# The first attention and the first plain feed-forward of a network of eight steps, put into one order of work written out by hand

## The chip, the core and the metric

The kernel runs on one core of a Trainium2 chip. A core has TensorE for matrix products (its weight loads are shown as PEld), VectorE (DVE), ScalarE (ACT), GpSimd (POOL) and the queues that issue transfers. Each engine works through its own list of instructions in order, and waits where an operand is not there yet. The metric is the device time of one execution in microseconds; less is better. Three runs of the kernel before took 3157.12, 3162.74 and 3170.88 us.

## The reference

The input is a tensor `x` of 2 batches, 1024 tokens and 256 channels in float32. Eight steps add to it in turn:

```python
x = x + attn_a(layernorm(x))     # 16 query heads, 8 key heads of 32, soft cap
x = x + ffn0(layernorm(x))       # 256 -> 512 -> 512 -> 256, relu
x = x + attn_b(layernorm(x))     # 16 query heads, 4 key heads of 16
x = x + ffn0(layernorm(x))       # the same weights again
x = x + attn_d(layernorm(x))     # differential attention
x = x + ffn1(layernorm(x))       # quantized weights
x = x + ttt(layernorm(x))        # a recurrence over chunks of 16 tokens
x = x + ffn1(layernorm(x))
```

Only the first two lines are touched by the change. The attention projects the normalized tokens to queries, keys and values, turns queries and keys by a rotary table, and forms for every head

```python
att = softmax(where(causal, 50 * tanh(q @ k.T / 16 / 50), -inf))
y = (att @ v) @ Wo
```

The feed-forward is `relu(relu(h @ W1.T + b1) @ W2.T + b2) @ W3.T + b3`.

## The kernel before

`build` (L1763) loads `x` (16 tiles of 128 tokens) and all weights of the first four steps at the start, on the queues of SP and ScalarE, and then runs the list `STAGES` (L1760): the first attention, the feed-forward, the second attention, the feed-forward again, and so on. The feed-forward `ffn0` is one function, called twice.

**The attention** (`attn_a`, L310, and `attn_a_chunk`, L360). The work is cut into four chunks: for each batch the first 512 queries (c = 0) and the last 512 (c = 1). The manual order of `in_order` (L277) makes TensorE, VectorE, ScalarE and GpSimd follow the order in which the code is written. A chunk consists of rounds, one for each pair (u, r) of head groups and each block kb of 128 keys. Four heads are worked at a time, on four row groups of TensorE. Chunk c = 0 has 16 rounds, chunk c = 1 has 32, and in the last four rounds of each head group only 512, 384, 256 and 128 query columns are left by the causal mask.

A round has three parts. `scores` (L424) forms four score products (L431) into two PSUM tiles of two banks, then ScalarE takes tanh (L437) out of PSUM and exp (L442) in place, in two halves, and GpSimd zeroes what the mask forbids (L445) where the block lies on the diagonal. `weigh` (L450) forms the products of the weights with v (L456) into the PSUM bank `py`, and VectorE adds the weights to a running sum `acc` (L466 to L473). At the last block of a head group `finish` (L478) forms row sums with a column of ones (L483), and VectorE turns, divides and turns back (L488 to L494) into `yT`.

Between the rounds stand pieces: the inputs of the next chunk and the outputs of the chunk before. The inputs of a pair of tiles are the layernorm in three steps (`token_inputs`, L293: `stats` and `rows` on VectorE with scalings on GpSimd, L196 and L205; `turn` with transposes on TensorE, L220, and a copy on VectorE, L223), then for each tile `queries`, `keys`, `turn_queries` and `turn_keys`: a projection (L232), the rotary products on VectorE (L259, L268) and their sum on GpSimd (L273), transposes (L396, L405) and copies (L397, L406). The outputs are four products with Wo (L411), each added to `x` on VectorE (L416). `spread` (L282) gives each round a number of pieces by its columns. The loop at L342 issues for round n: its scores, one piece, the products with v of round n−1, the finish of round n−2 if it was the last of its group, and the remaining pieces.

PSUM has eight banks here: four for the score tiles, two for the pieces (tag `g`), one for `py` and one for the row sums (`sm`).

**The feed-forward** (`ffn0`, L520) starts when the attention has ended, and its order is left to the planner. `layernorm_T` (L137) takes statistics of eight tiles (L146, L147), a square root on ScalarE (L148), scales on VectorE (L154), transposes on TensorE (L160) and copies on both engines in turn. Then, for each quarter of 512 tokens, two hidden layers of four blocks each (products L537 with two and four steps; relu with bias on ScalarE, L541) and four outputs (L546), added to `x` on VectorE (L551), with the bias b3 added on GpSimd (L552).

**The second attention** (`attn_b`) allocates its own memory and PSUM, clears some of it on GpSimd (L574 to L587), takes its first two tiles through a layernorm, and goes on in an order of its own.

Of the kernel before, what the change touches and what calls it, by code (L numbers as in the profile page):

```python
# [44 lines left out]
class Net:  # L45
# [235 lines left out]

    def spread(self, weights, pieces):  # L282

        total, at, out = sum(weights), 0.0, []
        done = 0
        for w in weights:
            at += w
            upto = round(len(pieces) * at / total)
            out.append(pieces[done:upto])
            done = upto  # L290
        return out
# [18 lines left out]
    def attn_a(self, w, wo, cos, sin):  # L310
# [6 lines left out]
        with ExitStack() as ctx:  # L317
# [8 lines left out]
            for b in range(B):  # L326


                kT = big.tile([P, 2, T], F32, tag="kT", name="kT", bufs=2)
                v = big.tile([P, NB, 8, 32], F32, tag="v", name="v", bufs=2)  # L330
                chunks += [self.attn_a_chunk(pools, b, c, kT, v) for c in range(2)]
            for step in chunks[0].inputs:
                step()
            rounds, fill = [], []
            for n, chunk in enumerate(chunks):
                inputs = chunks[n + 1].inputs if n + 1 < len(chunks) else []
                outs = chunks[n - 1].outputs if n else []
                pieces = []
                interleave_into(pieces, inputs, [lambda: None] * 2 + outs if outs else [])
                fill += self.spread([r.columns for r in chunk.rounds], pieces)  # L340
                rounds += chunk.rounds
            for n in range(len(rounds) + 2):  # L342
                here, last, ended = (
                    rounds[n - j] if 0 <= n - j < len(rounds) else None for j in range(3)
# [6 lines left out]
                if last:  # L351
                    last.weigh()
# [4 lines left out]
            for step in chunks[-1].outputs:  # L357
                step()

    def attn_a_chunk(self, pools, b, c, kT, v):  # L360
# [7 lines left out]
        def bank(name):  # L368
            return ps.tile([P, 512], F32, tag="g", name=name, bufs=2)

        def queries(j, made):
            if j == 0:
                shared["qT"] = big.tile([P, 2, 2, 512], F32, tag="qT", name="qT", bufs=2)
                shared["yT"] = big.tile([P, 4, 512], F32, tag="yT", name="yT", bufs=2)
# [3 lines left out]
            qr = roped["q"] = work.tile([P, 2, 2, 4, HD], F32, tag="qr", name="qr")  # L378
# [5 lines left out]
        def keys(j, made):  # L384
# [3 lines left out]
            kr = roped["k"] = work.tile([P, NKV, HD], F32, tag="kr", name="kr")  # L388
            self.rope(work, pkv[:, 0:256], NKV, HD, cos[:, i, :], sin[:, i, :], True,
                      [(kr, lambda t: t)], "rq", 2)  # L390
            nc.vector.tensor_copy(v[:, i], pkv[:, 256:512].rearrange("p (h d) -> p h d", d=HD))

        def turn_queries(j):
            pt = bank("t_ps").rearrange("p (n q) -> p n q", q=P)
            for n in range(4):
                nc.tensor.transpose(pt[:, n, :], roped["q"][:, n // 2, n % 2], self.ident)  # L396
# [4 lines left out]
        def turn_keys(j):  # L401
            i = 4 * c + j
            pt = bank("t_ps").rearrange("p (n q) -> p n q", q=P)
            for u in range(2):
                nc.tensor.transpose(pt[:, u, :], roped["k"][:, 4 * u : 4 * u + 4, :], self.ident)  # L405
            nc.vector.tensor_copy(kT[:, :, i * P : (i + 1) * P], pt[:, 0:2])  # L406
# [11 lines left out]
        def round_(u, r, kb):  # L418
# [5 lines left out]
            def scores():  # L424
# [4 lines left out]
                for s in range(4):  # L429
                    rows = slice(32 * s, 32 * s + 32)  # L430
                    nc.tensor.matmul(  # L431
                        tiles[s // 2][:, s % 2, 0:m], kT[rows, u, kb * P : (kb + 1) * P],
# [17 lines left out]
            def weigh():  # L450
# [4 lines left out]
                for s in range(4):  # L455
                    nc.tensor.matmul(  # L456
                        py[32 * s : 32 * s + 32, off:512], v[:, kb, 4 * u + s, :],
# [16 lines left out]
                if kb == end:  # L474
                    own.turned = work.tile([P, 16, 32], F32, tag="tny", name="turned")
                    nc.vector.transpose(own.turned.rearrange("p n d -> p (n d)"), py)

            def finish():  # L478


                sm = ps.tile([P, 512], F32, tag="sm", name="sm")
# [23 lines left out]
        chunk.outputs = [lambda j=j: output(j) for j in range(4)]  # L505
        chunk.inputs = []
        for p in range(2):
            made = {}
            i = b * NB + 4 * c + 2 * p
            chunk.inputs += self.token_inputs(work, bank, (i, i + 1), made)  # L510
            for j in (2 * p, 2 * p + 1):
                chunk.inputs += [
                    lambda j=j, m=made: queries(j, m), lambda j=j, m=made: keys(j, m),
                    lambda j=j: turn_queries(j), lambda j=j: turn_keys(j),
# [1398 lines left out]
```

## Time and profile before

| what | value |
| --- | --- |
| runs of the kernel before | 3157.12, 3162.74, 3170.88 us |
| the profiled execution, its time | 3170.71 us |
| its span, first to last instruction | 3168.9 us |
| mean granted clock of TensorE | 0.89 of full speed |
| first attention, first scores to last output | 55.1 to 431.4 us |
| first feed-forward, to its last product | 431.7 to 555.9 us |
| first transposes of the second attention | 563.0 us |

A line of TensorE's or another engine's timeline gives the start, the length, the engine, the line of the code and the operation with its result and operands; "x8" means eight instructions in a row, merged. A float32 product is two instructions in the trace, so a round's four score products show as eight. A line of waits gives the engine and the line that waited, what ended the wait, the total in microseconds, how often, and the longest. "PE py L456 <- POOL pr L445" is TensorE, at the products with v, standing idle until GpSimd's mask was done. In the view by stretches each engine has its busy time and, in brackets, the number of its instructions. Matrix products overlap in the record, so the distance from one start to the next tells more of their cost than their lengths.

### The profile page before, as it was taken

The page shows a single profiled execution, that of the slowest core. Times are in us where ns is not written, and L with a number is a line of the kernel's source. Part 1 is how long each engine was busy: PE and PEld are TensorE (multiplying, and loading weights), DVE is VectorE, ACT ScalarE, POOL GpSimd, SP SyncE. Part 2 cuts the span into 40 slices and gives each one's busy share as a digit, 9 for nine tenths or more (in the row PEclk, how much of TensorE's full clock was granted, in tenths as well). Part 3 has the DMA queues.
Part 4 walks back from the last instruction along what each step waited for, and adds up shares of the span by engine and source line. Part 5 has one row for each costly group of instructions (what it writes and reads, how often), then busy time and mean ns, then how long its engine had stood idle before and what let it go on. Part 6 is the DMA issues. An engine that isn't in the chain of part 4 may idle for free.

```text
span 3168.9 us, 66877 instructions
## 1 busy us (share of the span) xinstructions
PE 2640.7 (83%) x26384; PEld 1622.8 (51%) x26384; DVE 1922.1 (61%) x6646; ACT 1355.2 (43%) x2713; POOL 1030.5 (33%) x1648
## 2 busy tenths in 40 slices
PE   6888889699997866978887878878867689889998
PEld 2233245343433433655655555555644567767777
DVE  4776650576765446666676867778615665665652
ACT  2785942144454334664655555656512121221210
POOL 2444210211203456566564655656500000000000
PEclk8999989799998975988989888898987699999999
DMA  3000000000001100000000000000001111001000
GB/s 111 1 1 1 1 1 0 1 1 1 1 1 27 47 8 1 1 1 1 1 1 1 1 1 1 1 1 1 1 18 22 30 23 22 10 22 36 22 10 14
DMA packets 61978, 35.38 MB, mean 11 GB/s; under 512 B 43216, under 2 KB 58080, under 8 KB 61664
## 3 DMA queue, kind: packets, MB, share of 16 engines
q1 hardware_dynamic: 59472, 29.49, 3.6%
q8 instruction: 208, 3.41, 0.4%
q10 hardware_dynamic: 2192, 1.61, 0.2%
q14 instruction: 106, 0.87, 0.1%
HBM read 22.68 MB, written 8.39 MB: 10 GB/s over the span
## 4 chain that ended last, share of the span: by engine, by line
PE 36%; DVE 13%; ACT 7%; issue 4%; POOL 3%; DMA 0%; POOLq 0%; DVEq 0%; ACTq 0%; SPq 0%
PE ph L1255 6%; PE po L1746 4%; DVE p L1057 4%; PE e L1046 4%; ACT p L1068 4%; PE pg L1733 4%; PE pu L1733 3%; PE dT L1105 3%; PE po L1272 2%; POOL p L1081 2%; DVE p L1094 2%; PE py L1122 1%; PE pa L1416 1%; PE kh L1416 1%; PE pq L1416 1%
## 5 line engine op out<-in xcount | busy, mean ns | idle before, releaser
L1057 DVE CUSTOM_DVE_ANT_0 p<-e,mask 128x512 f32<-128x512 f32 (+3 forms) x768 | 381.7, 553 | 106.4 <-PE e L1046 105.1
L1068 ACT ACTIVATE p<-p,nm 128x128 f32<-128x128 f32 (+7 forms) x512 | 389.9, 764 | 97.7 <-DVE nm L1057 88.1
L1081 POOL TENSOR_SCALAR p<-p,ra,neg_lam 128x128 f32<-128x128 f32 (+7 forms) x256 | 222.8, 870 | 235.6 <-DVE ra L1077 180.9
L1105 PE MATMUL dT<-ident,p 128*128 128x128 f32 x1152 | 200.5, 308 | 112.9 <-ACT pT L1109 29.7
L1109 ACT ACTIVATE pT<-dT 128x128 f32<-128x128 f32 (+7 forms) x256 | 165.5, 647 | 285.8 <-PE dT L1105 284.5
L1046 PE MATMUL e<-kT,qT 32*128 32x512 f32 (+3 forms) x1536 | 234.2, 625 | 28.0 <-DVE nm L1057 26.7
L196 POOL TENSOR_SCALAR ln_mv<-ln_mv 128x2 f32<-128x2 f32 x48 | 15.7, 328 | 739.9 <-DVE ln_mv L194 728.3
L1094 DVE CUSTOM_DVE_ANT_0 p<-p,rs 128x128 f32<-128x128 f32 (+7 forms) x256 | 207.8, 833 | 69.8 <-POOL p L1085 69.6
L1105 PEld LDWEIGHTS dT<-ident,p 128*128 128x128 f32 x1152 | 154.7, 158 | 173.2 <-POOL p L1085 49.5
L723 ACT ACTIVATE pr<-s 128x512 f32<-128x512 f32 (+3 forms) x384 | 157.1, 496 | 167.6 <-PE s L718 164.4
L1098 POOL TENSOR_SCALAR p<-p,md 128x128 f32<-128x128 f32 (+7 forms) x256 | 208.2, 813 | 25.4
L437 ACT ACTIVATE pr<-s 128x1024 f32<-128x1024 f32 (+1 forms) x192 | 146.1, 821 | 126.7 <-PE s L431 123.1
L1255 PE MATMUL ph<-xT,up 128*128 128x256 f32 x512 | 138.2, 419 | 20.0 <-DVE inter L1263 18.3
L683 PE MATMUL s<-kT,qT 32*128 32x512 f32 (+3 forms) x768 | 151.2, 531 | 2.3 <-ACT pr L723 1.3
L442 ACT ACTIVATE pr<-pr 128x1024 f32<-128x1024 f32 (+1 forms) x192 | 153.0, 861 | 0.0
L1255 PE MATMUL ph<-xT,gate 128*128 128x256 f32 x512 | 138.5, 417 | 15.8 <-ACT xT L225 10.8
L691 DVE CUSTOM_DVE_ANT_0 masked<-s,mask 128x128 f32<-128x128 f32 (+3 forms) x256 | 110.7, 487 | 55.0 <-PE s L683 54.6
L1746 PE MATMUL po<-down,inter 128*128 128x256 f32 x512 | 140.7, 437 | 2.2 <-DVE x L1753 1.2
L445 POOL TENSOR_SCALAR_AFFINE_SELECT pr<-pr 128x256 f32<-128x256 f32 x128 | 93.5, 747 | 146.0 <-ACT pr L442 84.4
L1733 PE MATMUL pg<-xT,gate 128*128 128x256 f32 x512 | 131.3, 401 | 7.5 <-ACT xT L225 5.5
L456 PE MATMUL py<-pr,v 128*32 128x512 f32 (+3 forms) x768 | 115.1, 541 | 26.6 <-POOL pr L445 24.6
L1255 PEld LDWEIGHTS ph<-xT,up 128*128 128x128 f32 x512 | 101.2, 207 | 62.3 <-DVE inter L1263 28.9
(301 smaller groups left out, 5440.1 us busy)
## 6 DMA issues: line engine op xcount, KB each, us to landing
uk_d<-uk SPq DMA_DIRECT2D x128, 32.0 KB, 1.8
r<-uk_d SPq DMA_DIRECT2D x8, 512.0 KB, 4.2
x<-in_L_attn_a_X SPq DMA_DIRECT2D x4, 512.0 KB, 6.1
qh_d<-qh SPq DMA_DIRECT2D x8, 256.0 KB, 2.7
o<-qh_d SPq DMA_DIRECT2D x128, 16.0 KB, 1.8
out<-x SPq DMA_DIRECT2D x4, 512.0 KB, 3.1
w<-in_L_ffn_W2T SPq DMA_DIRECT2D x1, 1024.0 KB, 7.9
pk<-in_L_ffn_gate_packed SPq DMA_DIRECT2D x8, 128.0 KB, 2.4
```

The source lines that it names most:

```text
L723: nc.scalar.activation(pr[:, g, off:512], tiles[g][:, 0:m], AF.Exp, scale=0.25)
L1046: nc.tensor.matmul(own.tiles[h][:, a, 0 : hi - lo], made["q"][r : r + 32, a, t, :], kT[r : r + 32, a, lo:hi], start=True, stop=True,)
L1057: nc.vector.tensor_tensor_reduce(own.p[h][a][:, lo:hi], own.tiles[h][:, a, 0 : hi - lo], neg_row[:, T - nk + lo : T - nk + hi], -1.0, 3e38 ...
L1068: nc.scalar.activation(own.p[h][a], own.p[h][a], AF.Exp, bias=own.nm[:, h, a : a + 1], scale=-1.0, accum_out=own.sm[:, h, a : a + 1],)
L1081: nc.gpsimd.tensor_scalar(p1, p1, own.ra[:, h : h + 1], nlam[:, head : head + 1], ALU.mult, ALU.mult)
L1094: nc.vector.tensor_tensor_reduce(p0, p0, p1, own.rs[:, h, 0:1], -3e38, ALU.add, ALU.max, md)
L1098: nc.gpsimd.tensor_scalar(p0, p0, md, 1.0, ALU.add, ALU.mult)
L1105: nc.tensor.transpose(dT[:, kb, :], own.p[h][0][:, kb * P : (kb + 1) * P], self.ident)
L1109: nc.scalar.activation(pT[:, 0 : qb + 1, :], dT[:, 0 : qb + 1, :], AF.Exp)
L1255: nc.tensor.matmul(ph[:, j, :], w[:, kc, m * P : (m + 1) * P], f.xT[:, kc, :], start=(kc == 0), stop=(kc == 1),)
L1733: nc.tensor.matmul(ph[:, j, :], m_[:, kc, m * P : (m + 1) * P], f.xT[:, kc, :], start=(kc == 0), stop=(kc == 1),)
L1746: nc.tensor.matmul(f.po[:, b], inter[m // 2][:, m % 2, b * P : (b + 1) * P], wd[:, m % 2, (m // 2) * C : (m // 2 + 1) * C], start=(m == 0) ...
```

## The change

The first attention and the first feed-forward become one function, `attn_a_ffn0`, in one order written out by hand, and the list of stages has one entry less. The feed-forward's second call stays as it was.

- The feed-forward is cut into 22 pieces for each quarter of 512 tokens (`ffn0_pieces`): twice stats, rows and turn of a pair of tiles (the bias b3 is added to `x` in rows, on GpSimd); four pieces of the first hidden layer; eight of the second, each with two of a block's four steps; four outputs. The layernorm is that of `token_inputs`, without ScalarE. Relu with bias is one VectorE instruction that adds and takes the maximum with 0.
- Every piece has a cost. `share` gives out the pieces of a chunk by cost, with weights of the rounds' columns plus 100. A first part of the next chunk's inputs goes to the first three rounds of a chunk; the rest, mixed with the outputs of the chunk before and the pieces of the feed-forward, to the others. The first quarter of the feed-forward stands in the second chunk, the second and most of the third in the fourth. Nine pieces of the third quarter, the outputs of the last chunk and the last quarter follow after the last round.
- The products with v of round n−2, not n−1, are issued in round n, and the finish of round n−3.
- The row sums lose their own PSUM bank, and the pieces have three banks instead of two, which the sums share.
- In the inputs of a pair of tiles the order is now queries 0, keys 0, queries 1, transposes of queries 0, keys 1, transposes of keys 0, of queries 1, of keys 1. Keys and values are kept per chunk instead of per batch, in three buffers.

The core of the diff:

```diff
-            for n, chunk in enumerate(chunks):
-                inputs = chunks[n + 1].inputs if n + 1 < len(chunks) else []
-                outs = chunks[n - 1].outputs if n else []
-                pieces = []
-                interleave_into(pieces, inputs, [lambda: None] * 2 + outs if outs else [])
-                fill += self.spread([r.columns for r in chunk.rounds], pieces)
+            for chunk, first, second, third in (
+                (chunks[0], chunks[1].inputs, [], []),
+                (chunks[1], chunks[2].inputs, chunks[0].outputs + after[0], []),
+                (chunks[2], chunks[3].inputs, chunks[1].outputs, []),
+                (chunks[3], after[1], chunks[2].outputs + after[2][:6], after[2][6:-held]),
+            ):
+
+                weights = [r.columns + 100 for r in chunk.rounds]
+                quota = sum(weights[:3]) / sum(weights) * sum(
+                    cost for cost, _ in first + second + third
+                )
+                n = 0
+                while n < len(first) and quota > 0:
+                    quota -= first[n][0]
+                    n += 1
+                fill += self.share(weights[:3], first[:n])
+                fill += self.share(weights[3:], mixed(first[n:], second) + third)
                 rounds += chunk.rounds
-            for n in range(len(rounds) + 2):
-                here, last, ended = (
-                    rounds[n - j] if 0 <= n - j < len(rounds) else None for j in range(3)
+            for n in range(len(rounds) + 3):
+                here, turned, ended = (
+                    rounds[n - j] if 0 <= n - j < len(rounds) else None for j in (0, 2, 3)
                 )
...
-                if last:
-                    last.weigh()
+                if turned:
+                    turned.weigh()
...
-            for step in chunks[-1].outputs:
+            rest = mixed(after[2][-held:], chunks[3].outputs + after[3][:6]) + after[3][6:]
+            for _, step in rest:
                 step()
...
+    def share(self, weights, pieces):
+        total, cost = sum(weights), sum(c for c, _ in pieces)
+        out, at, done, spent = [], 0.0, 0, 0.0
+        for n, w in enumerate(weights):
+            at += w
+            here = []
+            while done < len(pieces) and (
+                n == len(weights) - 1
+                or spent + pieces[done][0] / 2 <= cost * at / total
+            ):
+                spent += pieces[done][0]
+                here.append(pieces[done][1])
+                done += 1
+            out.append(here)
+        return out
...
+        def hidden(m, part, src, w, bias, dst):
+            n = w.shape[1]
+            if part == 0:
+                f.ph = bank("ph")
...
+            for kc in range(2 * part, 2 * part + 2):
+                nc.tensor.matmul(
+                    f.ph, w[:, kc, m * P : (m + 1) * P], getattr(f, src)[:, kc],
+                    start=(kc == 0), stop=(kc == n - 1),
+                )
+            if 2 * part + 2 == n:
+                nc.vector.tensor_scalar(
+                    getattr(f, dst)[:, m, :], f.ph, bias[:, m : m + 1], 0.0, ALU.add, ALU.max
+                )
...
+            return ps.tile([P, 512], F32, tag="g", name=name, bufs=3)
...
-                sm = ps.tile([P, 512], F32, tag="sm", name="sm")
+                sm = bank("sm")
...
+            for cost, f, *args in (
+                (1.75, queries, j, made), (1.75, keys, j, made), (1.75, queries, j + 1, made),
+                (0.6, turn_queries, j), (1.75, keys, j + 1, made), (0.35, turn_keys, j),
+                (0.6, turn_queries, j + 1), (0.35, turn_keys, j + 1),
+            ):
...
-STAGES = ["attn_a", "ffn0", "attn_b", "ffn0", "attn_d", "ttt"]
+STAGES = ["attn_a", "attn_b", "ffn0", "attn_d", "ttt"]
```

## The prediction

> **What bounds the kernel now.** I read the page's busy times first. TensorE is busiest, but an average over six stages says nothing of one stage, and the chain of the work that ended last breaks off at 1124.88 us, after the part that is changed. So I cut the trace where the change lies: the first attention runs from 55.10 us (first score product) to 431 us, the first feed-forward to 555.9 us (its last product), the second attention starts its first transposes at 563.0 us.
>
> ```profile
> span 3168.9 us, 66877 instructions
> PE 2640.7 (83%) x26384; PEld 1622.8 (51%) x26384; DVE 1922.1 (61%) x6646; ACT 1355.2 (43%) x2713; POOL 1030.5 (33%) x1648
> ```
>
> The view by stretches (busy time and count of TensorE, its weight loads, VectorE, ScalarE, GpSimd, then granted clock). Its first four lines are the four chunks (batch, half of the queries), bounded by the first score products of each.
>
> ```profile
> 55.00:119.00 64.00, 54.86 (x340) 19.34 (x342) 42.93 (x93) 40.33 (x64) 28.48 (x49) 0.89 0.00 1
> 119.00:239.50 120.50, 104.94 (x640) 35.58 (x640) 89.45 (x120) 100.50 (x128) 57.32 (x51) 0.94 0.00 1
> 239.50:311.00 71.50, 62.16 (x390) 25.24 (x392) 51.09 (x105) 40.22 (x64) 33.22 (x52) 0.93 0.00 1
> 311.00:421.00 110.00, 96.59 (x588) 29.93 (x591) 66.88 (x55) 99.30 (x128) 24.30 (x33) 0.96 0.00 1
> 421.00:431.70 10.70, 10.31 (x40) 6.86 (x40) 4.57 (x9) 0.00 (x0) 0.00 (x0) 0.81 0.00 0
> 431.70:441.00 9.30, 2.82 (x11) 1.64 (x11) 9.06 (x42) 2.47 (x4) 0.00 (x0) 0.69 0.00 0
> 441.00:559.50 118.50, 114.89 (x343) 63.78 (x342) 15.52 (x43) 23.66 (x35) 14.34 (x18) 0.98 0.00 1
> ```
>
> ScalarE (40, 100, 40, 99 us) bounds the long chunks but not the short ones, and none reaches its bound; the feed-forward is TensorE alone (115 of 118.5), with ScalarE and VectorE nearly free. TensorE's busy time is inflated by waits and a low clock, so its need must come from start to start at full clock. TensorE's timeline:
>
> ```profile
> 221.09 1.06 PE L456 MATMUL py<-pr,v 128*32 128x512 f32 x8
> 222.09 1.14 PE L431 MATMUL s<-qT,kT 32*128 32x512 f32 x8
> 223.16 1.99 PE L411 MATMUL po<-wao,yT 128*128 128x256 f32 x8
> 225.09 1.07 PE L456 MATMUL py<-pr,v 128*32 128x512 f32 x8
> ...
> 452.56 13.90 PE L537 MATMUL ph<-h,w 128*128 128x512 f32 x32
> ```
>
> A full round's product with v takes 1.00 us (221.09 to 222.09), its scores 1.07, one output 1.93. A hidden pass is 13.90/32 = 0.434, so four passes, one new piece, 1.74. From other starts of this view: a projection 1.92, a feed-forward output 1.73, the row sums 0.97, query and key transposes 0.58 and 0.37, transposes after a layernorm 0.6; scores of 384, 256, 128 columns 0.86, 0.64, 0.43, their products with v 0.78, 0.57, 0.36.
>
> The waits of 55 to 421 us say why the chunks miss their bounds:
>
> ```profile
> ACT pr L437 <- PE s L431: 123.1, 45, 44.7
> PE py L456 <- POOL pr L445: 24.6, 30, 1.4
> PE ln_t L220 <- POOL ln_xn L205: 15.7, 6, 3.8
> ```
>
> Of ScalarE's 123.1 us, 44.7 lie before the first round. TensorE itself stands 24.6 us for the causal mask of the round just before, and 15.7 us at six layernorms. Each of these leaves a low clock: at 61.45, transposes, products with v and projection take 1.15+1.87+2.94 us instead of 0.6+1.0+1.92.
>
> **What the Trainium skill says.** "TensorE: Matmul & The Clock Gate", "What's actually happening": an idle window of about 3.4 us halves the array's clock until a busy window has passed. The trace agrees: scores take 1.07 us warm and 1.90 (320.62 to 322.52) after gaps. "SBUF — State Buffer", "Who interferes with whom": a VectorE operation with two SBUF inputs blocks a GpSimd read. Agrees: the two layernorm scalings took 3.01 us at 132.05, beside a 2.29 us sum, against 1.09 alone at 562.39. "ScalarE: Activation LUTs", "What ACT_TABLE_LOAD costs": about 1283 ns for each change of set; the load at 435.39 took 1.28.
>
> **The change part by part**, against the profiled execution's span of 3168.9 us (its time 3170.71; the median of the runs, 3162.74, is 8 lower; I take the difference off the median).
>
> *Need of TensorE.* Rounds: a short chunk has four groups of scores 3.00, products 2.71, sums 0.97, together 26.7 us; a long one has four more full rounds of 2.07 in each group, 59.8. Inputs of a chunk: 8×1.92 + 4×0.95 + 2×0.6 = 20.4. Outputs: 7.7. A feed-forward quarter: 1.2 + 12×1.74 + 4×1.73 = 29.0. Distributing the pieces as the new code does: chunk 0 holds 26.7+20.4 = 47; chunk 1 59.8+20.4+7.7+29.0 = 117; chunk 2 55; chunk 3 59.8+7.7+29.0 and the third quarter less its nine held pieces, 13.4, = 110; the rest 15.6+7.7+29.0 = 52. Against ScalarE's 40, 100, 40, 99 TensorE is now the longer in each: 381 us in all. Before, the longer of the two was 47, 100, 55, 99, and the chunks took 64, 120.5, 71.5, 110: 65 us above.
>
> *What comes on top.* (a) Pieces are lumps: summing for every round the longer of its TensorE work (scores, pieces, products of two rounds back) and its ScalarE work gives 346 instead of 329 for the four chunks: 17. (b) Layernorms: 14 instead of 6. By the distribution, four chunks open with statistics, rows and transposes in the same gap; TensorE waits for about 1.2 (statistics) + 1.3 (a sum) + 1.8 (rsqrt) + 1.2 (scaling) less its own 1.6, near 3.8 us, plus 2.3 of low clock: 4×6 = 24. In three gaps rows and transposes stand side by side with a sum between, as at 132 us: 3+2.3 each, 16. The five others inside the rounds have a round between and cost about nothing, two in the rest 1.5 each. Sum 43. Queued behind such a transpose on TensorE are the products and the next scores, so ScalarE waits as well. (c) After the last round two products with v, sums and masks drain with nothing beside: 3. (d) The last quarter's joins (first hidden product after xT, outputs after the last relu): 2. (e) VectorE's lag, below: 6. Together 71, so 452 us from the first score product to the last feed-forward product, where before it is 555.9 − 55.1 = 501: **49 us gained**.
>
> *Products two rounds behind.* The 24.6 us at the mask go: by then ScalarE and GpSimd are a whole round past. This is in the sum, since no such wait is added. The cost is one more live `pr`; four buffers leave one round of margin, since the first of a group is read again with the second. The single `py` bank still waits for its transpose (0.41 to 1.14 us at some group ends), in (e).
>
> *Relu on VectorE.* 32 of 128x512 out of PSUM; the nearest row is VectorE's xT out of PSUM, 0.69 us (ScalarE's relu: 0.69). 22 us join VectorE, in chunk 1 with the quarter's layernorm and sums 14, beside some 86 us: 100 of 134. Hidden while VectorE keeps up; behind a relu stand the 2.3 us sums and the emptying of banks. Bounds: 0 if hidden; 0.69 each, 22, if none is. I take 6 with (e). One table load and the return to exp (2×1.28) and ScalarE's copies go: under other work or in the 9.3 us start of the feed-forward, which goes wholly (it is in the 501).
>
> *Third bank, shared with the sums; new order of inputs.* Before the first scores the two pairs of tiles stop at 27.84, 32.30, 32.98, 48.67, 53.20 for GpSimd's rope; with a projection or transpose put between, some 1.5 each pair: **3 us gained** (0 to 5).
>
> *Bias b3 on GpSimd* rides with the layernorm; 16×0.72 = 12 us on a half idle GpSimd, behind the scalings, ahead of masks now needed a round later: nothing, 0.7 each if the masks come late.
>
> *Into the second attention.* The gap 555.9 to 563.0 is GpSimd's: a b3 addition, then 5.7 us of memsets that waited for feed-forward memory. The addition is gone; the memsets may come earlier, but VectorE's statistics now come after the last output: some 5 us stay. **2 us gained** (0 to 5). No DMA is moved; SP and ScalarE's queues issue all weights by 25 us, the feed-forward first needs them after 119.
>
> Sum: 49+3+2 = **54 us**; 3162.7 − 54 = 3109.
>
> **The rivals.** *Fewer stalls, 3075*: VectorE runs ahead of TensorE and has the layernorms done when TensorE comes; (b) falls from 43 to some 15 and (a) to some 10, as a round of scores lies ready: 88. For it: VectorE has 20 to 30% free; against: the six layernorms before did stall under the same freedom. *Stalls again, 3136*: every one of the 14 layernorms costs about the 5 us of before (15.7/6 of waiting and 2.3 of low clock): 70 instead of 43, a gain of 27. For it: the same chain through VectorE and GpSimd stands in each; against: half of them have a round between. *No change within 0.5%* (16 us, about what a measurement of this kernel can tell): that, and slot waits on top. *Slower, 3180*: the three banks become the bound. Some 140 allocations, each released only by VectorE in order; if a bank comes late by 0.4 us on average (54/140), the gain is gone, and at 0.5 the kernel is slower by 17. A 2.29 us sum ahead of a release does that on every fifth; for it stands VectorE's 100 us in chunk 1, against it that two other pieces and a round, some 5 us, lie between use and reuse.
>
> **How the numbers follow.** Likeliest (gain 40 to 70): 0.58. Fewer stalls (70 to 100): 0.22. Stalls again (16 to 40): 0.12. Within 16 us: 0.05. Slower: 0.03. Range 3072 to 3142 (gain 91 to 21) leaves out part of the second and third and the last two, under 0.2. Faster 0.92, same 0.05, slower 0.03.
>
> **What would show it.** Right: the last product of the first feed-forward near 502 us; chunks of about 61, 134, 68, 126; no wait of py for the mask of note; waits of the layernorm transposes three or four long, at chunk starts; granted clock above 0.93 there; ScalarE near 280 us busy in 450. Wrong: waits of TensorE for VectorE at bank reuse (hidden products, projections behind relu or sums) above 20 us, or ScalarE waiting in full rounds of chunk 1 where TensorE has one piece only; or later stages that change by more than 5 us.

## The result, and the profile after

The kernel after takes 3142.24 us (median of 12 runs, 3134.18 to 3152.03), the kernel before on the same chip 3166.55 us (12 runs, 3157.12 to 3176.62). The ratio is 0.9924, with a 95% interval of 0.9907 to 0.994: about 24 us faster, between 19 and 29. The prediction was 3109 with a range of 3072 to 3142: right in sign, but its gain of 54 us is more than twice the measured one.

The head of the page of the kernel after (its profiled execution took 3135.49 us):

```profile
span 3133.8 us, 66937 instructions
PE 2600.8 (83%) x26384; PEld 1602.7 (51%) x26384; DVE 1948.2 (62%) x6736; ACT 1329.8 (42%) x2673; POOL 1046.1 (33%) x1672
```

Below, *the stage* is the time from the first score product to the last product of the first feed-forward. It was 55.10 to 555.89, 500.8 us; it is now 51.80 to 527.92, 476.1 us. The first transposes of the second attention moved from 563.0 to 534.34. So 28.7 us were gained by then: 24.7 in the stage, 3.3 ahead of it, and 0.7 in the gap behind it. The prediction had 49, 3 and 2.

The same view by stretches as before the change, cut at the first scores of the four chunks, at the last scores, and at the last product of the feed-forward (busy time and count of TensorE, its weight loads, VectorE, ScalarE, GpSimd, then the granted clock):

```profile
51.80:117.50 65.70, 50.12 (x329) 18.59 (x329) 41.32 (x92) 40.28 (x64) 27.91 (x50) 0.87 0.00 1
117.50:256.00 138.50, 126.32 (x728) 47.75 (x728) 98.88 (x159) 100.67 (x127) 55.37 (x58) 0.95 0.00 1
256.00:331.70 75.70, 60.89 (x388) 25.18 (x384) 48.17 (x103) 40.93 (x66) 28.93 (x52) 0.89 0.00 1
331.70:462.30 130.60, 121.13 (x694) 44.50 (x696) 87.78 (x127) 99.47 (x124) 46.77 (x48) 0.95 0.00 1
462.30:527.90 65.60, 59.46 (x208) 33.62 (x204) 26.33 (x59) 1.27 (x4) 9.98 (x15) 0.95 0.00 0
```

The pieces did go between the rounds of the long chunks, and TensorE works in 126 of 138 us there. But the two short chunks, which received nothing new, did not become shorter: 65.7 and 75.7 us, where 63.8 and 71.3 stood before, at granted clocks of 0.87 and 0.89. And the part after the last scores takes 65.6 us for pieces priced at 52.

TensorE's waits within the stage (engine and line, what ended the wait, total us, times, longest):

```profile
PE ln_t L220 <- POOL ln_xn L205: 29.9, 5, 7.5
PE ln_t L421 <- POOL ln_xn L205: 16.8, 6, 5.1
PE py L564 <- POOL pr L553: 3.9, 4, 1.2
PE s L539 <- DVE qT L506: 2.2, 2, 1.1
PE py L564 <- DVE turned L584: 1.3, 1, 1.3
PE s L539 <- ACT pr L545: 1.1, 2, 0.6
```

The mask waits of the products with v are nearly gone, 24.6 before and 3.9 now. The waits for a layernorm's scaled rows have tripled, from 15.7 us in six to 46.6 in eleven; a 6.5 us wait at the start of the old feed-forward is gone. Over the stage, waits went from 53.0 to 57.9 us and TensorE's running time, start to start less the waits, from 447.8 to 418.2. So by this view nothing of the waiting was gained. But the view counts a stop only where no product is on record as running, and a stop inside a group hides behind the products ahead of it. I priced every piece of both traces at the prediction's own start-to-start times, which gives 381 us in each, and sorted what is above the price by the granted clock of the piece. At a low clock (under 0.95) it is 24 us before and 25 after; at full clock 43 before and 13 after. Of the 43, 22 are in the products with v and 19 in the scores: the second pair of heads stands inside its group of eight for a mask, an exp or a tanh. After the change 1 and 4 of these are left, and that is the gain.

Why a layernorm is waited for so long is seen in the timeline of all engines in the first short chunk, at its second layernorm (start us, length, engine, line, operation; in brackets the idle time before and what ended it; rows picked from 83 to 91 us):

```profile
83.95 1.72 DVE L574 TENSOR_TENSOR acc<-pr 128x1536 f32<-128x1536 f32 x1
85.77 1.94 ACT L545 ACTIVATE pr<-s 128x1024 f32<-128x1024 f32 x2 [3.71 <-DVE acc L574]
87.50 0.16 DVE L184 SCALAR_TENSOR_TENSOR rsq_y<-rsq_w,rsq_y 128x2 f32<-128x2 f32 x1
89.66 0.41 POOL L553 TENSOR_SCALAR_AFFINE_SELECT pr<-pr 128x256 f32<-128x256 f32 x1 [0.53 <-ACT pr L550]
90.06 1.10 POOL L205 TENSOR_SCALAR ln_xn<-x,ln_mv,rsq_y 128x256 f32<-128x256 f32 x2
90.67 0.69 PE L220 MATMUL ln_t<-ident,ln_xn 128*128 128x128 f32 x2 [7.47 <-POOL ln_xn L205]
```

To be read from below. TensorE waits 7.47 us for the scaled rows. GpSimd scales at 90.06, though VectorE had the reciprocal root ready at 87.50 + 0.16 = 87.66: ahead of the scaling in GpSimd's list stand the two causal masks of the round just issued, and these wait for that round's exp. That exp is late because its tanh waited 3.71 us until 85.77 for a weights buffer, which VectorE's first sum frees. "PSUM — Partial Sum Buffer" of the Trainium skill, "Engine vs sequencer instructions", says that the lists of ScalarE, VectorE and GpSimd are strictly first in, first out; the trace agrees, with 90.06 − 87.66 = 2.4 us of a scaling that has its input and does not start. At the start of this chunk the scaling again stands behind two masks, though no tanh waited for a buffer: root ready at 55.16, second mask done at 57.28, scaling at 57.55, transposes at 58.16 after 5.22 us of waiting.

### The profile page after: what moved, and what is told of

Same layout as the page of the kernel before. It is cut to its first block, busy times and chain, and to the rows that moved or that the text cites. A ratio compares the mean times of both kernels' runs of the same rounds, so it can differ in the third digit from the quotient of the medians.

```text
span 3133.8 us, 66937 instructions
## 1 busy us (share of the span) xinstructions
PE 2600.8 (83%) x26384; PEld 1602.7 (51%) x26384; DVE 1948.2 (62%) x6736; ACT 1329.8 (42%) x2673; POOL 1046.1 (33%) x1672
## 4 chain that ended last, share of the span: by engine, by line
PE 36%; DVE 14%; ACT 7%; issue 4%; POOL 3%; DMA 0%; POOLq 0%; DVEq 0%; ACTq 0%; SPq 0%
PE ph L1367 7%; DVE p L1169 4%; PE po L1858 4%; PE e L1158 4%; ACT p L1180 4%; PE pg L1845 4%; PE pu L1845 3%; PE dT L1217 3%; PE po L1384 2%; POOL p L1193 2%; DVE p L1206 2%; PE py L1234 1%; PE pa L1528 1%; PE pq L1528 1%; PE kh L1528 1%
## 5 line engine op out<-in xcount | busy, mean ns | idle before, releaser
L196 POOL TENSOR_SCALAR ln_mv<-ln_mv 128x2 f32<-128x2 f32 x56 | 25.4, 453 | 778.5 <-DVE ln_mv L194 766.8
L1858 PE MATMUL po<-down,inter 128*128 128x256 f32 x512 | 135.4, 425 | 1.2 <-DVE x L1865 1.2
L1384 PE MATMUL po<-down,inter 128*128 128x256 f32 x512 | 129.2, 400 | 2.0 <-DVE x L1391 1.1
```

What stands on the lines that cost most here:

```text
L1384: nc.tensor.matmul(f.po[:, b], f.inter[:, m, b * P : (b + 1) * P], wd[:, m % 2, (m // 2) * C : (m // 2 + 1) * C], start=(m == 0), stop=(m ...
L1858: nc.tensor.matmul(f.po[:, b], inter[m // 2][:, m % 2, b * P : (b + 1) * P], wd[:, m % 2, (m // 2) * C : (m // 2 + 1) * C], start=(m == 0) ...
```

## The experiments

All readings of the stage are of one profiled execution each, and the first question is how far such a reading carries.

**The kernel after once more** (no edit).

> The kernel after, unchanged, to see how far one execution's readings of the stage carry. Stage length is first score product to last feed-forward product: 476.1 us in the first profile of it. If the readings of single profiles can be compared: 476 within 1.5 us, though the total may move by 5 or more. If they can't: a difference of 4 or more, and then the one-look results of this study (4 to 8 us apart) say nothing.

The stage took 476.5 us, 52.52 to 529.01, against 476.1. The waits for layernorms were 29.9 and 16.8 us again, and ScalarE waited for the first sums 17.5 us in 8 again. Times: 3146.94 us (4 runs), ratio 0.9923 (0.9896 to 0.9949). The two spans, 3133.8 and 3146.3, differ by 12.5 us, of which 11.5 lie in the last stage, the recurrence with its feed-forward: 775.2 and 786.8 us from its first product (2358.52 and 2359.51) to the end. So, as far as two executions tell, the stage can be compared to within a microsecond; a single total cannot, and from here on I compare stages and give times where there were several runs.

**No wait for the layernorm rows.** The transposes read a weight tile in place of the scaled rows; everything else is issued as before. The products thus work on other numbers: the normalized values are left out.

```diff
+            still = wo[:, 0:2, :]
...
+            self.still = still
...
-            made["xT"] = self.layernorm_turn(work, pt, made["xn"], False, True)
+            xn = getattr(self, "still", None) or made["xn"]
+            made["xT"] = self.layernorm_turn(work, pt, xn, False, True)
...
-                        pt[:, kc, j * P : (j + 1) * P], f.xn[:, j, kc * P : (kc + 1) * P],
+                        pt[:, kc, j * P : (j + 1) * P], self.still[:, j, kc * P : (kc + 1) * P],
```

> The transposes of every layernorm in the merged stage, except the two pairs before the first round, read a fixed tile of weights instead of the scaled rows; statistics, scalings and everything else stay and are paid for. The normalized values are left out, so only the waits can be read from it. Theory (layernorm chains are what came on top): TensorE's 46.6 us of waits for the scalings go, and some 2 us of low clock after each of ten, so the second attention's first transposes come 55 to 65 us earlier than the changed kernel's 534.3, at 470 to 480. Had the prediction's own size for them (43 us) been right: at about 491. Rival (VectorE's lag at the PSUM banks, or ScalarE, is what holds the stage): the waits only move, and it starts after 510.

The stage fell to 441.0 us (51.40 to 492.40), 35.1 less, at a mean granted clock of 0.97 where it was 0.93. TensorE's waits in it now:

```profile
PE pq L232 <- DVE xT L223: 9.8, 3, 5.6
PE s L544 <- ACT pr L550: 6.8, 7, 3.1
PE py L569 <- POOL pr L558: 5.9, 5, 2.0
```

The second attention's first transposes came at 498.8 us, later than the 470 to 480 of the theory and than the 491 of the prediction's own size. In the kernel after, the waits for layernorms are 46.6 us, and the pieces that follow them run another 22.8 us above their price at a low clock. Taking these waits away is worth only 35 us, since others come in their place: the projections wait 9.8 us for VectorE's copy behind the transposes (0.8 in the kernel after), and the scores wait 6.8 us for ScalarE (1.1) and another 11.7 inside their groups (4.0). TensorE still runs 413 us, 32 above the 381 that the prediction added up as its need: 12 at a low clock behind the other waits, 12 in scores that stop inside a group for tanh, and 7 in pieces of the feed-forward that take longer between rounds than in a row.

**Rows two rounds earlier.** Statistics and scaling of every layernorm between the rounds (the pieces marked `ahead`) are issued two rounds earlier, their transposes where they were.

```diff
+            ahead = 2
+            for n, pieces in enumerate(fill):
+                for piece in pieces:
+                    if getattr(piece, "ahead", False):
+                        (moved[n - ahead] if n >= ahead else start).append(piece)
```

> Same work, but statistics and rows of every layernorm between the rounds are issued two rounds earlier, the transposes stay. Theory: seven of the nine long waits between the rounds shrink to under 1 us; the second attention starts 30 to 45 us earlier than at 534.3, and the time is 30 to 45 us below the changed kernel's 3142. Rival (banks, VectorE): within 10 us of it.

The stage took 454.7 us, 21.4 less than after where 30 to 45 were expected, and the kernel 3132.68 us (4 runs), 0.9892 of before (0.9862 to 0.9921). TensorE's waits in the stage:

```profile
PE ln_t L220 <- POOL ln_xn L205: 15.2, 4, 4.4
PE s L557 <- DVE qT L524: 7.9, 2, 3.9
PE ln_t L436 <- POOL ln_xn L205: 4.3, 3, 1.6
```

Waits for layernorms fell by 27.2 us, from 46.6 to 19.5; the others rose by 7.5, most of it at the first scores of a chunk, which now wait for the copy of the queries. This edit changes neither the work nor the number of the engines' instructions, only where two pieces stand. The four waits that are left in L220 are those of the short chunks.

**Masks last.** The masks of a round are issued after the round's pieces, so that a scaling stands ahead of them in GpSimd's list.

```diff
+            def masks():
+                for h in range(2):
                     if kb >= 4 * c:
-                        d = halves[h][:, :, 0:P]
+                        d = own.halves[h][:, :, 0:P]
...
                 for piece in pieces[1:]:
                     piece()
+                if here:
+                    here.masks()
```

> The causal masks of a round are issued on GpSimd after the round's pieces instead of before them, so that a scaling does not queue behind a mask that waits for this round's exp. Theory (in the short chunks the scaling stands behind two masks): the waits of 5.2, 7.5, 4.7 and 7.4 us there lose 1.5 to 3 us each, the start at 534.3 comes 6 to 12 us earlier. Rival (the chain through VectorE is what is late): under 2 us. A new wait of the products with v for masks would show as a loss.

The stage stayed at 476.7 us; one run took 3149.68 us. The mechanism is there: the first layernorm waited 3.00 us instead of 5.22, the second 6.45 instead of 7.47, all of them 42.0 instead of 46.6. But the products with v waited 8.2 us for masks instead of 3.9. The order of masks and scalings alone thus is a real cause of the long waits at two places and worth nothing in the whole: the wait moves. A scaling that is early helps, one that pushes a mask aside does not.

**The attention's edits alone.** The new attention with its three banks, two rounds of distance and new order of inputs, but no feed-forward pieces between the rounds; then the old feed-forward.

```diff
-                (chunks[1], chunks[2].inputs, chunks[0].outputs + after[0], []),
+                (chunks[1], chunks[2].inputs, chunks[0].outputs, []),
...
-                (chunks[3], after[1], chunks[2].outputs + after[2][:6], after[2][6:-held]),
+                (chunks[3], [], chunks[2].outputs, []),
...
-            rest = mixed(after[2][-held:], chunks[3].outputs + after[3][:6]) + after[3][6:]
+            rest = chunks[3].outputs
```

> The new attention (products two rounds behind, three shared banks, new order of inputs, pieces by cost) without any piece of the feed-forward, which follows afterwards in its old form. Theory: the attention's own edits gain about the 20 us of mask waits and 3 of the start, less what longer layernorm waits at chunk starts and ScalarE's waits for the first sum take, so last output some 5 to 15 us before 431; the time lies between the two kernels, 3150 to 3160. Rival (the attention's edits bring all, the merge nothing): 3142. Second rival (they bring nothing or lose, the merge brings all): 3166 or more.

It is slower than before, as the second rival had it: 3186.72 us (6 runs), ratio 1.0061 (1.004 to 1.0082). The stage took 510.6 us, 9.8 more than before; the attention within it, first scores to last output, 386.9 instead of 376.3. TensorE's waits in the attention:

```profile
PE ln_t L220 <- POOL ln_xn L205: 27.8, 6, 7.5
PE s L539 <- ACT pr L545: 16.4, 22, 2.0
PE py L564 <- POOL pr L553: 10.0, 9, 1.9
```

Before, these three were 15.7, 4.2 and 24.6: 44.5, and now 54.2. With fewer pieces between the rounds, the time that TensorE no longer stands at the mask it stands one step later, at the scores, where ScalarE's tanh has not freed the bank; and the same six layernorms wait 12 us longer. So the merge as such is worth 510.6 − 476.1 = 34.5 us of the stage, and the rest of the edits take 10 of it back. Which of them does so is shown in part only, by the next run; the new order of inputs and the sharing by cost were not run alone.

**One round behind.** The products with v of round n−1 in round n, as before the change; all else as after.

```diff
-                    rounds[n - j] if 0 <= n - j < len(rounds) else None for j in (0, 2, 3)
+                    rounds[n - j] if 0 <= n - j < len(rounds) else None for j in (0, 1, 2)
```

> The changed kernel with the products with v one round behind the scores again, the finish two. Prediction's step (24.6 us of waits for masks are worth their whole length): the second attention's first transposes, at 534.3 in the changed kernel, come 20 us or more later, and TensorE waits some 20 us for masks. Theory after the run of the attention alone (the waits were mostly traded for waits of the scores for ScalarE): mask waits return, but ScalarE's 17.5 us of waits for the first sum go, and the start moves by less than 10 us.

The stage took 472.2 us: 3.9 less than with two rounds, where the prediction's step had it 20 or more longer. The mask waits are 11.9 us in 11, not 24.6. ScalarE's waits for sums within the chunks, first of the kernel after, then of this one:

```profile
ACT pr L545 <- DVE acc L574: 17.5, 8, 3.7
```

```profile
ACT pr L545 <- DVE acc L574: 2.7, 3, 1.0
```

With one round of distance the first weights of a group are summed a round earlier and their buffer is free in time. The second layernorm of a short chunk, 7.47 and 7.36 us after, waits 4.57 and 4.42. That is the chain shown above, cut at its last link.

**First weights copied.** The first weights of a group go into the sum as a copy, so that their buffer is not read again with the second, and the sums are issued behind the finish of their round; two rounds of distance stay. VectorE moves more data for it.

```diff
-                if kb == 1:
-                    acc = shared["acc"] = work.tile(
...
+                if kb == 0:
+                    shared["acc"] = work.tile([P, 4, 512], F32, tag="acc", name="acc", bufs=1)
+                    nc.vector.tensor_copy(shared["acc"], pr)
```

> The first weights of each head group are copied into the running sum with their own products, one round before, instead of being added to the second ones; so a buffer of weights comes free a round earlier, for 16 copies on VectorE of about 1.1 us. Theory (ScalarE's tanh waits 17.5 us for that buffer, and in the short chunks masks and scaling wait behind it): these waits go, two layernorm waits of 7.4 lose 3 us each, start at 534.3 earlier by 5 to 12 us. Rival (TensorE is the pace, ScalarE's wait is hidden): within 3 us, or later by VectorE's added work.

The stage took 479.6 us, 3.5 more. ScalarE's waits for sums fell only from 17.5 to 9.4 (plus 3.5 at the other sums, as after), and the layernorm waits stayed at 47.0. Freeing the buffer by a copy on VectorE buys nothing, and that it is the longer list of VectorE which takes the gain back is argued, not shown.

**Relu on ScalarE.** The 32 relus are ScalarE activations with bias again, between the rounds.

```diff
-                nc.vector.tensor_scalar(
-                    getattr(f, dst)[:, m, :], f.ph, bias[:, m : m + 1], 0.0, ALU.add, ALU.max
-                )
+                nc.scalar.activation(
+                    getattr(f, dst)[:, m, :], f.ph, AF.Relu, bias=bias[:, m : m + 1]
+                )
```

> Relu with bias by ScalarE again, all else as changed. Prediction's step (VectorE's lag costs 6 us, up to 22 by relu): the start at 534.3 comes 0 to 6 us earlier. Rival (ScalarE's order is worse: a relu stands behind tanh and exp of a whole round, up to 3.7 us, and the bank comes late): 5 to 20 us later.

The stage took 468.5 us, 7.6 less. The four chunks are the same within 1 us (65.9, 139.2, 76.2, 129.4 against 65.7, 138.5, 75.7, 130.1); all of it lies after the last scores, 57.9 instead of 66.1. TensorE there, first after (from 461.83), then with this edit (from 464.32):

```profile
465.30 0.77 PE L564 MATMUL py<-pr,v 128*32 128x256 f32 x8 [1.25 <-POOL pr L553]
467.01 0.41 PE L564 MATMUL py<-pr,v 128*32 128x128 f32 x4 [0.93 <-POOL pr L553]
469.51 2.85 PE L435 MATMUL ph<-h,w 128*128 128x512 f32 x4
```

```profile
466.39 0.77 PE L564 MATMUL py<-pr,v 128*32 128x128 f32 x8 [0.36 <-POOL pr L553]
468.48 1.98 PE L435 MATMUL ph<-h,w 128*128 128x512 f32 x4
```

The drain of the last rounds takes 7.7 us with relu on VectorE and 4.2 without, and the first hidden piece after it runs at full clock, 1.82 us to the next start instead of 2.69. A relu itself takes 0.75 us on VectorE and 0.69 on ScalarE. Further on, in the kernel after, a relu on VectorE waits 1.94 us for TensorE's product until 486.18, and behind it in VectorE's list stands the reciprocal root of the next layernorm, at 486.84, for whose rows TensorE then waits 1.50 us; with this edit that layernorm is in time. "ScalarE: Activation LUTs", "Rules for kernel authors", advises VectorE for relu; at this place ScalarE is the better one, being idle there (1.27 of 65.6 us busy after the change), and the measurement decides. The trace shows no table load of ScalarE in this stage.

**Two banks and one for the sums**, as before the change.

```diff
-                return ps.tile([P, 512], F32, tag="g", name=name, bufs=3)
+                return ps.tile([P, 512], F32, tag="g", name=name, bufs=2)
...
-                sm = bank("sm")
+                sm = ps.tile([P, 512], F32, tag="sm", name="sm")
```

> Two banks for the pieces and one for the row sums, as before, instead of three shared. Prediction's slower rival (the banks can become the bound): with two, TensorE waits at pieces, start at 534.3 later by 5 to 20 us. Rival (banks were never short): within 3 us.

The stage took 477.0 us, 0.9 more: the third bank is worth about nothing in it. The first scores came at 55.21 instead of 51.80, and at 50.68 to 53.74 in all the kernels of this study with three banks. So by this one reading the third bank, and not the new order of inputs, which this kernel keeps, gives the start its 1.5 to 4.5 us.

**Combinations**: rows two rounds earlier together with one round of distance, with relu on ScalarE, and with both.

> Layernorm rows two rounds early and products with v one round behind. The two were worth 21.4 and 3.9 us of the stage alone. If the waits are separate (layernorms on GpSimd's and VectorE's queues, freeing of weights' buffers on ScalarE's): stage 449 to 453 us. If the second is only a smaller form of the first, because ScalarE late means masks late means rows late: 454 or more, and mask waits of 10 to 15 us are added.

> Layernorm rows two rounds early and relu back on ScalarE. Alone the relu was worth 7.6 us of the stage. If relu on VectorE costs by itself (it delays sums, and with them buffers for ScalarE): stage 445 to 449 us. If it costs only as one more thing ahead of a layernorm's statistics, rows two rounds early have taken that already: 452 to 456.

> All three: rows two rounds early, products one round behind, relu on ScalarE. If the three are separate: stage 441 to 446 us, the time about 3108 to 3115 us, the best so far. If they share their cause: not below 450, time as that of rows two rounds early alone.

| kernel | stage, us | time, us (4 runs) | ratio to before, interval |
| --- | --- | --- | --- |
| after, again | 476.5 | 3146.94 | 0.9923 (0.9896 to 0.9949) |
| rows early, one round behind | 455.4 | 3124.31 | 0.9855 (0.9824 to 0.9886) |
| rows early, relu on ScalarE | 449.2 | 3118.84 | 0.984 (0.9814 to 0.9866) |
| all three | 449.3 | 3119.8 | 0.9837 (0.9804 to 0.987) |

The relu adds 5.5 us to the gain of the early rows, most of its 7.6. One round of distance adds nothing to it, 455.4 against 454.7, which fits that its 3.9 us came through the layernorm rows: these are no longer late. With it the mask waits are back (17.8 and 16.6 us) and the layernorm waits lower (10.3 and 8.7 against 19.5 and 18.0), one for the other. The version with early rows and relu on ScalarE beats both kernels: 28 us under the kernel after and 50 under the kernel before, both measured beside it.

## Why the prediction was right in sign and wrong in size

*The sum, term by term.* The prediction had 381 + 71 = 452 us for the stage, and 476 were measured. The same terms in the trace of the kernel after, by the prediction's own prices as above (its 43 for layernorms are 27 of waits and seven times 2.3 of low clock):

| term | predicted, us | in the trace, us |
| --- | --- | --- |
| need of TensorE | 381 | 381 |
| (b) waits for layernorms | 27 | 46.6 |
| (b) low clock behind these waits | 16 | 22.8 |
| (a) lumps: TensorE held by ScalarE at the scores, before a group (1.1) or inside it (4.0) | 17 | 5.1 |
| (c), (d), (e): drain, joins, VectorE's lag; all other waits and low clock | 11 | 12.0 |
| feed-forward pieces longer between rounds than in a row | 0 | 7.4 |

About 1 us of the 476 is left over.

*The step that failed* is (b), the layernorms, where 43 us were taken and 69 stood, 46.6 of them waits instead of 27. Four at chunk starts were priced at 3.8 each, and are 5.22, 5.08, 4.73 and 5.09. Three with rows and transposes side by side were priced at 3, and are 7.47, 7.36 and 2.84. The five inside the rounds were priced at nothing, and two of them waited 3.65 and 2.52. The two in the rest, at 1.5 each, were right (1.50 and 1.17). The working of this step added VectorE's statistics, a sum, the root and the scaling, as if the scaling began when its input is there. It left out GpSimd's list: at the second layernorm of a short chunk the scaling stands behind the masks of the round just issued, which wait for exp, and exp for tanh, and tanh for a buffer that a sum of VectorE frees. Where no mask stands in between, in the long chunks' starts, it was VectorE's list: at 117.3 a first sum in two operations, 1.74 and 0.41 us, was ahead of the statistics, and a further 1.19 us sum ahead of the root. The masks alone do not carry it: issued last, they took only 4.6 us off the waits. That the place in the lists costs, and not the length of the pieces, is shown by the same pieces issued two rounds earlier: waits of 19.5 us instead of 46.6, and a stage 21.4 us shorter.

*Waits that lie on top of each other were added.* Without the layernorms' waits the stage is 35 us shorter and not 69, and TensorE is then held by ScalarE for 6.8 + 11.7 = 18.5 us, close to the 17 of the lumps. So the lumps exist, but while layernorms are waited for they hardly show; that ScalarE catches up during those waits is argued, not shown.

*A reading that was wrong.* The prediction took the scores of 1.90 us at 320.62, in the kernel before, for a low clock after gaps. ScalarE's and TensorE's timelines there, the second half of these scores by itself, and the view by stretches:

```profile
319.45 1.96 ACT L437 ACTIVATE pr<-s 128x1024 f32<-128x1024 f32 x2
320.62 1.97 PE L431 MATMUL s<-qT,kT 32*128 32x512 f32 x8
321.46 1.13 PE L431 MATMUL s<-qT,kT 32*128 32x512 f32 x4
```

```profile
320.62:322.52 1.90, 1.90 (x10) 0.59 (x9) 1.90 (x1) 1.90 (x3) 0.00 (x0) 1.00 0.03 9
```

The granted clock is 1.00. The second pair of heads starts at 321.46, when the tanh of the round before has left its banks (319.45 + 1.96 = 321.41), and the two pairs, which take 1.07 us together, run one after the other. This is ScalarE's hold, and before the change it was worth 19 us at the scores, unseen among the waits. A low clock is seen at 61.45, where 0.50 was granted, and after a wait of 2.27 us, shorter than the idle window of about 3.4 us that the prediction cites. The 1283 ns that it gives for a change of ScalarE's set of functions are the load alone; the page that it cites counts a drain of about 1380 ns besides. Nothing was priced by it.

*"The 24.6 us at the mask go"* was true of the wait and false of the time. In the attention alone the wait went to the scores and to the layernorms, and the attention became 10.6 us longer; in the merged kernel one round of distance is even 3.9 us shorter. The prediction said of the two rounds that they cost one more live buffer and leave a round of margin. That margin was the error: the first buffer of a group is released with the second sum, and ScalarE stood 17.5 us for it.

*The need of 381 us* was nearly right. What it misses is plain in TensorE's timeline of the kernel after:

```profile
204.50 1.14 PE L539 MATMUL s<-qT,kT 32*128 32x512 f32 x8
205.57 1.98 PE L435 MATMUL ph<-h,w 128*128 128x512 f32 x4
207.48 1.06 PE L564 MATMUL py<-pr,v 128*32 128x512 f32 x8
...
240.58 1.99 PE L447 MATMUL po<-w,h 128*128 128x256 f32 x8
242.50 1.14 PE L539 MATMUL s<-qT,kT 32*128 32x512 f32 x8
...
507.11 13.90 PE L435 MATMUL ph<-h,w 128*128 128x512 f32 x32
```

A hidden piece between rounds takes 1.91 us from start to start (205.57 to 207.48), where the prediction took 4 × 0.434 = 1.74 from an unbroken row such as the last line shows. "TensorEngine Tiling (Array Packing)", "Key Properties", says that a change of tiling mode drains the array; the rows agree in so far as 0.17 us appears just where the tile goes from 32 rows or 32 columns to 128 and back. An output of the feed-forward takes 1.92 (240.58 to 242.50) and was priced at 1.73, also from a row, though the attention's output, of the same shape, stood in the prediction at 1.93 between rounds. Together this is 7.4 us. The scores sum to 95 us instead of 82; of the 13, 8 ran at a low clock behind layernorms and 4 are stops inside a group. The prediction's 33 us for low clock and lumps stand against 418.2 − 381 = 37 of running time above the need, and that this is so near is luck: the clock was taken 9 us too small, the lumps inside the groups 13 too large, and the longer pieces were absent.

*Relu on VectorE* was taken at 6 us within VectorE's lag, with bounds of 0 and 22, and is worth 7.6. The size was right and the place wrong: it cost nothing in chunk 1, where the prediction looked, and all of it after the last scores, where ScalarE is idle: 3.5 us in the drain and the rest behind it. The drain, (c), was for this reason priced too low: it took 7.7 us for some 3 us of products, nearly 5 on top where 3 were taken.

*The start* (3 predicted, 3.3 in the profile) was right, and is the third bank's by the one run that shows it. *The gap* into the second attention gave 0.7 of its 2. *The rest of the kernel* took 6.5 us less in the profile, which need not be the change's: between the two executions of the kernel after, that part differs by 11.4.

*The rivals.* "Stalls again, 3136" came nearest, and by its own price: it took 70 us for fourteen layernorms, waits and low clock together, and 69 stood in the trace, though not in equal parts: three waited not at all, and two over 7 us. It was given a chance of 0.12. The slower rival fell: the three banks are no bound, no wait for a bank's release among the leading waits, and a bank less costs 0.9 us.

## What to carry to other kernels

When a wait is removed by more distance, ask what the next thing in every in-order list is: here the distance freed TensorE from the mask and made ScalarE wait for a buffer, GpSimd's scaling for the masks behind ScalarE, and TensorE for the scaling. Price a chain over several engines by what stands ahead of each link in its engine's list, not by the lengths of its links; work that depends on nothing recent, such as statistics and scaling of rows long finished, should be issued rounds before its use. Price a short piece by its pitch among its new neighbours: a row of equal products shows a shorter one. Do not add up holds that can lie on top of each other. And look inside a group of products before taking its length for a slow clock: the granted clock of the stretch tells the two apart.

## What the runs showed that was not expected

The stage repeats to 0.4 us and its waits to 0.1 us between two executions, while the last stage, untouched, differs by 11.5 us. The view by stretches of most of its first half, of the kernel after and of its repeat:

```profile
2385.00:2700.00 315.00, 256.83 (x6713) 199.03 (x6713) 201.41 (x971) 64.01 (x152) 14.49 (x28) 0.84 0.10 22
```

```profile
2386.00:2700.00 314.00, 253.53 (x6546) 195.42 (x6544) 197.09 (x949) 61.58 (x148) 14.52 (x28) 0.81 0.10 22
```

The slower execution gets through fewer products (6546 in 314 us against 6713 in 315) at a granted clock of 0.81 instead of 0.84. A gain of a few microseconds in one stage of such a kernel is seen in the stage of one profile, and in totals only over many runs.
